# The very last store of an adaLN block, from one DMA queue to two

## Chip, core and metric

The kernel runs on one core of one Trainium2 chip (trn2). The metric is the device time of one execution in microseconds (us). Three runs of the kernel before took 598.09, 598.38 and 598.5 us; the median is 598.38 us.

## What is computed

The reference is a block with adaptive layer norm, in float32. The input x has 2 x 2048 tokens of 512 features, and each of the two sequences has one condition vector t.

```python
emb = jnp.dot(silu(t), ada_w) + ada_b
shift_msa, scale_msa, gate_msa, shift_mlp, scale_mlp, gate_mlp = jnp.split(emb, 6, axis=-1)
norm = _ln(x) * (1.0 + scale_msa[:, None]) + shift_msa[:, None]
h = gelu(jnp.dot(norm, ssm_w1) + ssm_b1, approximate=False)       # 512 -> 512
x = x + gate_msa[:, None] * (jnp.dot(h, ssm_w2) + ssm_b2)         # 512 -> 512
norm2 = _ln(x) * (1.0 + scale_mlp[:, None]) + shift_mlp[:, None]
hf = gelu(jnp.dot(norm2, ff_w1) + ff_b1, approximate=True)        # 512 -> 1024
x = x + gate_mlp[:, None] * (jnp.dot(hf, ff_w2) + ff_b2)          # 1024 -> 512
return x
```

`_ln` is the layer norm without weights: subtract the mean, multiply by the reciprocal root of the variance plus 1e-6.

## The kernel before, in words

The 4096 tokens are cut into eight blocks of 512 (`NBLK`), four to a sequence. Block i lies in SBUF as `xs[i]`, 128 partitions x 4 tokens x 512 features: partition p holds four consecutive tokens, so that a store of one token place c for all partitions writes one piece of each partition's row. The output is seen in the same way through `out_blk[i]`.

The four matrix products of each block run on TensorE by schemes that need fewer multiplications than the plain one. The products that end in a residual (`residual`, named `oA` for the first and `oC` for the second) are of Strassen's kind: seven half-sized products P1 to P7, made by `group` in the order P1, P2, P6, P5, P7, P3, P4 (`ORDER`), each of 2 x `kdim` matmuls of 128 columns by 256 (`kdim` is 4 in `oC`, so 16 matmuls per product). They accumulate in PSUM, partly on top of one another, and after each product the closure `after` lets VectorE add what stands in PSUM to a quarter of `xs[i]` (line 652). A quarter is two of the four token places by one half of the features.

The whole order of work is written out by hand (`manual_schedule`): the code issues instructions for each engine in the order of the program, and small pieces of other work (`hooks`) are placed behind chosen products. Each engine works through its own list, and waits on semaphores for the others. DMAs are issued by SyncE (queue q1 in the profile) and ScalarE (queue q10). ScalarE's DMAs are the first rows of constants, one quarter of a weight, and half of the exchange of transposed blocks (line 524). All stores of the output are SyncE's.

For blocks 0 to 6 the output is stored in two halves of 512 KB by `store` (line 675). For the last block (`last=True` in `residual`) the end is cut finer. P1, P6, P7 and P4 are taken apart by j (`parted`): the matmuls of j = 0 go to one PSUM tile and those of j = 1 to another, and `after` runs for each, with `js` the slice of one token place. Behind P7 the token places 2 and 3 of the upper half of the features are final and are stored one after the other, behind P3 the first two token places are stored by `store`, and behind P4 the token places 2 and 3 of the lower half of the features. That gives four stores of 128 KB from line 656 (128 partitions x 1 KB each), the last of which follows the last matmul and the last addition of the kernel. At the very end, the closing instructions of the program (line 1154) let SyncE wait for every DMA and bring all engines together.

Of the kernel before, what the change touches and what calls it, by code (L numbers as in the profile page):

```python
# [140 lines left out]
def kernel(  # L141
# [16 lines left out]
    nc = tc.nc  # L158
    P = 128
# [24 lines left out]
    out_blk = out.flatten_outer_dims().rearrange("(i p c) d -> i p c d", p=P, c=C)  # L184
# [230 lines left out]
    def group(name, kdim, lhs, rhs, after, hooks, parted=(), order=ORDER):  # L415

        ps = {}
        for p in order:  # L420
            b = BANK[p]
            fresh = b not in ps
            apart = p in parted
            if fresh:
                ps[b] = [
                    ps_g.tile([P, 2, HT], F32, tag=b, name=f"p{b}_{name}_{n}") for n in range(1 + apart)
                ]
            for j in range(2):
                for k in range(kdim):
                    nc.tensor.matmul(  # L430
                        ps[b][j * apart][:, j, :],
                        lhs(p, j, k),
                        rhs(p, j, k),
                        start=(fresh and j * (not apart) == 0 and k == 0),
                        stop=(p in ("P2", "P3", "P4") and k == kdim - 1),
                        skip_group_check=True,
                    )
                if apart:
                    after(p, {b: ps[b][j]}, slice(j, j + 1))
            if not apart:  # L440
                after(p, {b: ps[b][0]}, slice(0, 2))
            for op in hooks.get(p, ()):
                op()
# [194 lines left out]
    def residual(name, i, hops, wops, kdim, hooks, last=False, order=ORDER):  # L638

        xt = xs[i]  # L640
        F = D // 2
        q = {
            "11": xt[:, 0:2, :F],
            "12": xt[:, 0:2, F:],
            "21": xt[:, 2:4, :F],
            "22": xt[:, 2:4, F:],
        }
        dest = {"P1": "11", "P2": "11", "P6": "12", "P5": "22", "P7": "22", "P3": "12", "P4": "21"}

        def after(p, ps, js):  # L650
            d = q[dest[p]][:, js]
            nc.vector.tensor_tensor(d, ps[BANK[p]][:, js], d, ALU.add)  # L652
            if last and p in ("P7", "P4"):
                s = slice(2 + js.start, 2 + js.stop)
                f = slice(F, D) if p == "P7" else slice(0, F)
                nc.sync.dma_start(out=out_blk[i][:, s, f], in_=xt[:, s, f])

        parted = ("P1", "P6", "P7", "P4") if last else ()
        group(name, kdim, hops, lambda p, j, k: wops[p][:, k, :], after, hooks, parted, order)
# [499 lines left out]
```

## Time and profile before

| what | value |
|---|---|
| median of three runs | 598.38 us |
| the profiled execution's own time | 598.25 us |
| its span, first to last instruction | 596.2 us |
| TensorE busy (PE) | 589.3 us, 99% |
| VectorE, GpSimd, ScalarE busy | 373.0, 396.0, 219.8 us |
| granted TensorE clock | 1.0 |
| DMA queues q1 (SyncE) and q10 (ScalarE) | 45.11 MB and 4.22 MB |
| stores of 128 KB at line 656 | 4, each 332 to 333 ns to issue |
| ScalarE's last activation | starts 569.37 us, 0.91 us |

All times of the trace are microseconds from the start of the span. The span and the execution's own time differ by what lies around the instructions. A line of the timeline gives the start, the duration, the engine and line, the operation with the tiles it writes and reads, and in square brackets how long the engine had been idle and what ended that. Lines with "x2" merge two instructions, from the start of the first to the end of the last. SPq and ACTq are the instruction streams of SyncE and ScalarE; a DMA issue there is only the issue, and the bytes move later, on 16 DMA engines.

### The profile page before, as it was taken

The page shows a single profiled execution, that of the slowest core. Times are in us where ns is not written, and L with a number is a line of the kernel's source. Part 1 is how long each engine was busy: PE and PEld are TensorE (multiplying, and loading weights), DVE is VectorE, ACT ScalarE, POOL GpSimd, SP SyncE. Part 2 cuts the span into 40 slices and gives each one's busy share as a digit, 9 for nine tenths or more (in the row PEclk, how much of TensorE's full clock was granted, in tenths as well). Part 3 has the DMA queues.
Part 4 walks back from the last instruction along what each step waited for, and adds up shares of the span by engine and source line. Part 5 has one row for each costly group of instructions (what it writes and reads, how often), then busy time and mean ns, then how long its engine had stood idle before and what let it go on. Part 6 is the DMA issues. An engine that isn't in the chain of part 4 may idle for free.

```text
span 596.2 us, 8228 instructions
## 1 busy us (share of the span) xinstructions
PE 589.3 (99%) x2847; PEld 509.6 (85%) x2847; DVE 373.0 (63%) x638; ACT 219.8 (37%) x365; POOL 396.0 (66%) x465
## 2 busy tenths in 40 slices
PE   7999999999999999999999999999999999999997
PEld 4788888888888888888888888888888888888886
DVE  4978988897564475555754458653665246468642
ACT  3234437305432364133721356232553234212420
POOL 2878489999753994649968499966974695440200
PEclk9999999999999999999999999999999999999999
DMA  8990323200224004340042601321020300022001
GB/s 322 409 364 11 80 72 87 91 36 35 72 70 140 3 1 139 110 139 2 18 141 67 215 3 44 98 72 70 1 69 3 111 32 1 1 63 80 1 0 71
DMA packets 23481, 49.86 MB, mean 84 GB/s; under 512 B 4450, under 2 KB 5006, under 8 KB 22544
## 3 DMA queue, kind: packets, MB, share of 16 engines
q1 hardware_dynamic: 20400, 45.11, 22.5%
q10 hardware_dynamic: 3040, 4.22, 2.8%
q8 instruction: 23, 0.38, 0.3%
q14 instruction: 18, 0.15, 0.1%
HBM read 26.25 MB, written 8.39 MB: 58 GB/s over the span
## 4 chain that ended last, share of the span: by engine, by line
PE 97%; DMA 2%; DVE 1%; SPq 0%; issue 0%
PE py_oC L430 19%; PE px_hC L751 10%; PE py_oA L430 9%; PE pv_oC L430 9%; PE py_hA L430 9%; PE py_hC L751 8%; PE pv_hC L751 8%; PE pv_oA L430 5%; PE px_oC L430 5%; PE pv_hA L430 4%; PE py_hC L430 2%; PE px_oA L430 2%; PE px_hA L430 2%; DMA ada<-in_L_cond_ada_w_dram 2%; PE pv_hC L430 1%; PE pt L533 1%
## 5 line engine op out<-in xcount | busy, mean ns | idle before, releaser
L664 POOL TENSOR_TENSOR x<-x,gb 128x512 f32<-128x512 f32 x64 | 79.4, 1273 | 6.1 <-DVE gb L671 2.3
L547 ACT ACTIVATE nT<-nT,mod,mod 128x512 f32<-128x512 f32 x54 | 39.6, 802 | 105.3 <-DMA nT<-blocks 99.1
L473 POOL TENSOR_SCALAR ve<-mv 128x4 f32<-128x4 f32 x16 | 3.7, 230 | 91.3 <-DVE mv L465 85.2
L504 ACT ACTIVATE nT<-x,nmr,rstd 128x512 f32<-128x512 f32 x56 | 42.4, 803 | 51.6 <-POOL nmr L491 35.8
L430 PE MATMUL py_oC<-fw,hClo 128*128 128x256 f32 x256 | 57.9, 379 | 0.0
L430 PEld LDWEIGHTS py_oC<-fw,hClo 128*128 128x128 f32 x256 | 48.6, 190 | 6.6
L652 DVE TENSOR_TENSOR x<-py_oC,x 128x512 f32<-128x512 f32 (+1 forms) x36 | 22.6, 629 | 42.4 <-PE py_oC L430 42.4
L350 POOL TENSOR_TENSOR hSC<-hClo,hChi 128x512 f32<-128x512 f32 (+1 forms) x17 | 20.1, 1188 | 39.9 <-ACT hChi L746 29.2
L464 DVE BATCH_NORM_STATS2 st<-x 128x6 f32<-128x512 f32 x64 | 43.4, 678 | 5.0 <-DMA x<-in_x_dram 4.8
L751 PE MATMUL py_hC<-forms,fw 128*128 128x256 f32 x168 | 40.8, 379 | 0.0
L768 DVE TENSOR_TENSOR hClo<-hClo,py_hC 128x512 f32<-128x512 f32 x42 | 28.4, 680 | 16.9 <-ACT hClo L765 10.4
L515 DVE STREAM_TRANSPOSE blocks<-nT 128x512 f32<-128x512 f32 x56 | 37.8, 694 | 1.3 <-ACT nT L504 0.9
L689 POOL TENSOR_TENSOR forms<-forms 128x256 f32<-128x256 f32 x48 | 35.6, 741 | 2.8
L751 PEld LDWEIGHTS py_hC<-forms,fw 128*128 128x128 f32 x168 | 31.8, 190 | 4.4
L768 DVE TENSOR_TENSOR hChi<-hChi,pv_hC 128x512 f32<-128x512 f32 x35 | 23.3, 683 | 17.1 <-PE pv_hC L751 17.1
L652 DVE TENSOR_TENSOR x<-py_oA,x 128x512 f32<-128x512 f32 x32 | 22.0, 688 | 18.9 <-PE py_oA L430 18.3
L430 PE MATMUL py_hA<-nT,w 128*128 128x256 f32 x128 | 30.4, 380 | 0.0
L746 ACT ACTIVATE hClo<-hClo,colsT 128x256 f32<-128x256 f32 x56 | 25.4, 500 | 10.8 <-DVE hClo L768 10.7
L430 PE MATMUL py_oC<-fw_s,hSC 128*128 128x256 f32 x128 | 28.9, 379 | 0.0
L430 PE MATMUL pv_oC<-fw,hSC 128*128 128x256 f32 x128 | 28.9, 379 | 0.0
L430 PE MATMUL pv_oC<-fw_s,hSC 128*128 128x256 f32 x128 | 28.9, 379 | 0.0
L430 PE MATMUL py_oC<-fw_s,hChi 128*128 128x256 f32 x128 | 28.9, 379 | 0.0
(217 smaller groups left out, 1424.9 us busy)
## 6 DMA issues: line engine op xcount, KB each, us to landing
nT<-blocks SPq DMA_DIRECT2D x168, 64.0 KB, 2.0
out_dram<-x SPq DMA_DIRECT2D x15, 512.0 KB, 2.6
x<-in_x_dram SPq DMA_DIRECT2D x7, 1024.0 KB
ada<-in_L_cond_ada_w_dram SPq DMA_DIRECT2D x6, 1024.0 KB, 15.8
fw<-in_L_cond_ff_w_dram SPq DMA_DIRECT2D x3, 2048.0 KB
nT<-blocks ACTq DMA_DIRECT2D x56, 64.0 KB, 2.0
w<-in_L_cond_ssm_w_dram SPq DMA_DIRECT2D x3, 1024.0 KB, 9.5
x<-in_x_dram SPq DMA_DIRECT2D x2, 512.0 KB, 4.0
```

What stands on the lines that cost most here:

```text
L350: eng.tensor_tensor(out[:, r], a[:, r], b[:, r], f)
L430: nc.tensor.matmul(ps[b][j * apart][:, j, :], lhs(p, j, k), rhs(p, j, k), start=(fresh and j * (not apart) == 0 and k == 0), stop=(p in (" ...
L464: nc.vector.bn_stats(st, xs[self.i][:, c, :])
L504: nc.scalar.activation(t, x_c, AF.Identity, bias=self.nmr[:, c : c + 1], scale=self.rstd[:, c : c + 1])
L515: nc.vector.transpose(self.bl[:, :, :, c, :].rearrange("p m k q -> p k m q"), self.nT[:, c, :].rearrange("p (k m q) -> p k m q", k=KD, m=C),)
L547: nc.scalar.activation(dst, src, AF.Identity, bias=shift, scale=scale)
L652: nc.vector.tensor_tensor(d, ps[BANK[p]][:, js], d, ALU.add)
L664: lambda c=c: nc.gpsimd.tensor_tensor(xs[i][:, c, :], xs[i][:, c, :], gb, ALU.add)
L689: eng.tensor_tensor(reg[d], reg[a], reg[b], ALU.add if f == "+" else ALU.subtract)
L746: nc.scalar.activation(h, h, AF.Gelu_apprx_tanh, bias=fb1T[:, m : m + 1])
L751: nc.tensor.matmul(ps[b][:, j, :], fa[ra][:, j * P : (j + 1) * P], fb[rb].rearrange("p a (c q) -> p c a q", q=Q), start=(fresh and j == 0) ...
L768: nc.vector.tensor_tensor(dest(d), dest(d), ps[b], op)
```

## The change

The store behind P7 and the first of the two behind P4 stay as they are. The second one behind P4 (`js.start` is 1: the last store of all) becomes two stores of 64 partitions x 1 KB: partitions 0 to 63 issued by SyncE, partitions 64 to 127 issued by ScalarE. Both wait for the same addition of VectorE. No other instruction is added, removed or moved; all later lines of the code are numbered 5 higher (656 becomes 661, 675 becomes 680, 1154 becomes 1159).

```diff
             if last and p in ("P7", "P4"):
                 s = slice(2 + js.start, 2 + js.stop)
                 f = slice(F, D) if p == "P7" else slice(0, F)
-                nc.sync.dma_start(out=out_blk[i][:, s, f], in_=xt[:, s, f])
+
+                queues = (nc.sync, nc.scalar) if p == "P4" and js.start else (nc.sync,)
+                n = P // len(queues)
+                for e, eng in enumerate(queues):
+                    r = slice(e * n, (e + 1) * n)
+                    eng.dma_start(out=out_blk[i][r, s, f], in_=xt[r, s, f])
```

## The prediction

> **What bounds the kernel now.** I read the page first: the busy row of TensorE, and the chain that ended last.
>
> ```profile
> span 596.2 us, 8228 instructions
> PE 589.3 (99%) x2847; PEld 509.6 (85%) x2847; DVE 373.0 (63%) x638; ACT 219.8 (37%) x365; POOL 396.0 (66%) x465
> ...
> PE 97%; DMA 2%; DVE 1%; SPq 0%; issue 0%
> ```
>
> TensorE is busy for 99% of the span and 97% of the chain is matmul. The change touches none of that: it rewrites one DMA behind the last matmul. So only the tail can move, and I read the end of the timeline next (start, duration, engine, line).
>
> ```profile
> 589.16 3.62 PE L430 MATMUL py_oC<-fw_s,hChi 128*128 128x256 f32 x16
> ...
> 591.54 2.06 SPq L656 DMA_DIRECT2D out_dram<-x  x2
> 592.82 0.42 DVE L652 TENSOR_TENSOR x<-py_oC,x 128x256 f32<-128x256 f32 x1 [1.30 <-PE py_oC L430]
> ```
>
> The last addition ends at 592.82 + 0.42 = 593.24. The two merged stores end at 591.54 + 2.06 = 593.60, and one issue takes 332 ns, so the last store is issued from 593.27. The tail from there is 596.23 - 593.27 = 2.96 us, 0.5% of the span. I cut it by the DMA's own rows (each line: stretch, length, busy time by engine, clock, DMA share, GB/s), and look at what SyncE waits for at the very end and where the closing instructions of the program (line 1154) stand.
>
> ```profile
> 593.27:593.60 0.33, 0.00 (x0) 0.00 (x0) 0.00 (x0) 0.00 (x0) 0.00 (x0) 1.00 0.00 0
> 593.60:594.10 0.50, 0.00 (x0) 0.00 (x0) 0.00 (x0) 0.00 (x0) 0.00 (x0) 1.00 0.00 0
> 594.10:594.55 0.45, 0.00 (x0) 0.00 (x0) 0.00 (x0) 0.00 (x0) 0.00 (x0) 1.00 0.83 291
> 594.55:595.15 0.60, 0.00 (x0) 0.00 (x0) 0.00 (x0) 0.00 (x0) 0.00 (x0) 1.00 0.00 0
> 595.15:596.23 1.08, 0.00 (x0) 0.00 (x0) 0.00 (x0) 0.00 (x0) 0.00 (x0) 1.00 0.00 0
> ```
>
> ```profile
> SPq L1154 <- DMA out_dram<-x: 1.5, 1, 1.5
> ```
>
> ```profile
> L1154 SPq EVENT_SEMAPHORE  x7: 17/28/28, 595.2 to 596.2; - x7
> L1154 POOLq EVENT_SEMAPHORE  x4: 17/17/17, 595.6 to 596.1; - x4
> ```
>
> So the tail is: 0.33 issue, 0.50 until the first byte moves, 0.45 in which 128 KB move, 0.60 until SyncE is told, 1.08 of closing waits and the barrier of all engines. Only 0.45 us of it depends on bytes. A perfect halving of that would be worth 0.22 us, or 0.04% of the time.
>
> **The change part by part.** Before the tail nothing moves: on TensorE, VectorE and GpSimd the order of instructions is the same but for line numbers, SyncE has the same stores up to the last, and ScalarE has two instructions more, at its end.
>
> *SyncE's half.* One store of 128 partitions becomes one of 64, waiting on the same addition. Taken at the same 0.33 issue and 0.50 start-up: on SyncE the 512 KB store at 590.08 and the 128 KB stores have the same issue time (332 ns), so bytes do not set it. Whether fewer partitions shorten it no row shows for a store; the nearest, a 32-partition copy quoted below, has a longer issue (about 0.5 us) and moves its first byte 1.17 us after it begins, not earlier. So I take nothing saved. The other end: if the 0.50 halved with the partitions, 0.25 us saved. The form differs, so that end stays in the range.
>
> *ScalarE's half.* ScalarE ends its last activation at 569.37 + 0.91 = 570.28 and is then idle, so its wait for the addition holds up nothing but its own closing branch, drain and barrier signal, for which GpSimd collects from 595.6 on. ScalarE's issue would end by about 594.2 even at the longest of the rows below (0.86 us), so 1.4 us cover it; without that cover each us would be a us of time. Its wait is a semaphore instruction of its own followed by the DMA, as in SyncE's store of the addition at 585.91, which ends at 586.33 and whose store issues at 584.67 + 2.06 - 0.33 = 586.40: 0.07 after the addition, against 0.03 for the last store. So ScalarE issues 0.04 later, about 593.31.
>
> *The two together.* The trace has a place where SyncE and ScalarE issue in the same moment: the exchange of the transposed blocks, 64 KB each. First the timeline, then the DMA queues of the two next stretches, 532.12 to 532.44 and 532.44 to 532.76.
>
> ```profile
> 530.95 1.15 SPq L524 DMA_DIRECT2D nT<-blocks  x2
> 530.96 1.42 ACTq L524 DMA_DIRECT2D nT<-blocks  x2
> ```
>
> ```profile
> q1 hardware_dynamic: 34, 0.06, 76.6%
> ```
>
> ```profile
> q10 hardware_dynamic: 33, 0.06, 84.9%
> q1 hardware_dynamic: 14, 0.00, 5.4%
> ```
>
> From 530.9 to 532.12 no packet moves. Then q1 (SyncE's) moves its 64 KB in 0.32 us, and ScalarE's q10 moves none until 532.44. Issued 0.01 later, it starts 0.32 later. The pair at 179.16 and 179.17 shows the same: q1 from 180.33, q10 from 180.65. ScalarE's second issue is stretched too: the two SyncE issues take 512 and 583 ns, the two of ScalarE 523 and 864.
>
> Here the Trainium skill speaks against the change. Its page "DMA: Bandwidth & Descriptors", section "Rules for kernel authors", says not to bother with two transfers to disjoint partition halves, since both use the same 16 engines and their packets only interleave. By that rule the sum is 128 KB over the same engines: the same 0.45 us, and a difference of 0 to +0.04 us from ScalarE's later issue. The row says a little worse: no interleaving, one behind the other. If the 0.32 us is a delay in starting the second transfer, ScalarE's half starts at 594.10 + 0.32 = 594.42 and takes half of 0.45, so it ends at 594.64, which is 0.09 us behind the 594.55 of before. If the 0.32 us is only the time that the first one's bytes took, the wait scales with SyncE's half (0.22) and the end stays at 594.55. The rows don't separate these. I take +0.09, because the row is this very pair of queues, and the stretched second issue speaks for a shared step ahead of the bytes. The bounds: -0.25 (start-up scales with partitions), and 0.09 + (0.864 - 0.523) = +0.43 if ScalarE's half also meets the stretched issue.
>
> *The closing waits.* SyncE's list of waits has the same length; it waits first on the semaphore that ScalarE's half now counts, then on its own. The 1.08 us follow whichever lands last, so I cost this at nothing. It is a plain addition to the path: nothing covers a later landing.
>
> **Sum.** The profiled execution took 598.25 us, its span 596.23, with 2.02 us around it. 598.25 + 0.09 = 598.34. It lies 0.13 below the median of 598.38, so on that scale the forecast is 598.47, rounded to 598.5.
>
> **The rivals.** *It does nothing* (the halves interleave, as the rule has it): 598.38 to 598.42. For it: bytes and engines are the same. Against it: the 0.32 us of the row.
>
> *It helps*: with 64 partitions per queue the 0.50 us ahead of the first byte shortens, down to 598.38 - 0.25 = 598.13. For it: this stretch is dead time in which two queues might work at once. Against it: the 32-partition copy starts no sooner. To win over 0.2% (1.2 us) it would have to remove more than a third of a tail of which the closing 1.08 and the landing's 0.60 are not touched; hardly possible.
>
> *ScalarE's half meets the stretched issue*: 598.38 + 0.43 = 598.81. For it: the 864 ns. Against it: that was a second issue, and here there is one per queue.
>
> *Slower by over 0.2%: ScalarE's new instructions are not at hand when the addition ends.* The page's instruction queue, q8, has 23 packets that take 0.3% of 16 engines' span: 0.003 x 16 x 596.2 / 23 = 1.24 us each. A fetch is itself a transfer; with the 0.60 us that a store needs to be told, I estimate 1.24 + 0.60 = 1.84 us. If it fell between ScalarE's wait and its issue, the issue would come at 593.31 + 1.84 = 595.15, the first byte 0.83 later at 595.98, the last at 596.20: 1.65 us behind 594.55, or 600.0 us. It decides from the point where ScalarE issues later than 594.42 - 0.83 = 593.59; from there each us counts in full. Against it: ScalarE has 23 us of idle time before, and VectorE's closing drain is listed at the same 592.8 as its last addition, so it passed from the one to the other without a fetch.
>
> **How the numbers follow.** Second half delayed by a start-up, +0.09: 0.50. Nothing, 0 to +0.04: 0.27. A gain of up to 0.25: 0.13. Stretched issue, up to +0.43: 0.05. A fetch or another late arrival of ScalarE, about +1.65: 0.05. The runs of before spread over 598.09 to 598.5, about 0.2 either way. The range reaches from 598.13 less this spread, about 598.0, to 598.81 plus it, 599.0. A measurement of this kernel can tell about 0.2% (1.2 us) from no change; all but the last case lie within that. Slower by more: 0.05. Faster by more: 0.01, taken from the gain case for what I overlook. Within: 0.94.
>
> **What would show it.** In the profile after: TensorE's last matmul and VectorE's last addition at the same times as before within the spread (else something moved that I say does not). Two issues of line 661, on SPq at about 593.27 and on ACTq at about 593.31, with some 0.33 us each. No byte before 594.10; q1 with 64 KB first, q10 with 64 KB from 594.42 if the start-up is shared, both from about 594.10 if they interleave; the last byte near 594.6. SyncE's closing wait ends near 595.2 and the closing instructions take 1.08 as before. The prediction is wrong if the first byte comes clearly sooner than 0.83 after the issue, if ScalarE issues later than 593.59, or if the closing part grows, for instance through ScalarE arriving at the barrier after 595.6.

## The result and the profile after

The changed kernel takes 599.1 us in the median of 22 runs (598.67 to 601.39), the kernel before 598.49 us in 22 runs beside it: 0.61 us more. The ratio is 1.0016 with a 95% interval of 1.001 to 1.0022. That is slower, by less than the 0.2% that I had set as the bound of a change, and 0.1 us above the upper end of my range. A repeat on another occasion (e12 below) gave 1.0011, 1.0002 to 1.0019. The ratio of 1.0016 is more than 0.61 us would make (1.0010), since 7 of these 22 runs were a microsecond or more longer, at a granted clock of 0.997, as by their times were 2 of the 22 of before; in the repeat 1 run of 14 showed that clock.

The two profiled executions took 599.0 us (span 596.90) and 598.25 us (span 596.23). The page after says as before that TensorE is the chain.

```profile
span 596.9 us, 8230 instructions
...
PE 97%; DMA 2%; DVE 1%; SPq 0%; issue 0%
```

The end of the timeline after:

```profile
592.88 0.42 DVE L652 TENSOR_TENSOR x<-py_oC,x 128x256 f32<-128x256 f32 x1 [1.30 <-PE py_oC L430]
593.39 0.55 ACTq L661 DMA_DIRECT2D out_dram<-x  x1
```

The last addition ends at 593.30, 0.06 later than before, within the spread of runs. From there to the end of the span before took 596.23 - 593.24 = 2.99 us, and after it takes 596.90 - 593.30 = 3.60. The difference of 0.61 us is the whole loss, and it lies behind the last addition. This stretch, from the end of the last addition to the end of the span, is what I call the tail below. The issues of the stores after, from the view of the tensor `out_dram` (minimum, median and maximum in ns):

```profile
L661 SPq DMA_DIRECT2D out_dram<-x x4: 332/332/538, 584.7 to 593.3; - x4
...
L661 ACTq DMA_DIRECT2D out_dram<-x x1: 552/552/552, 593.4 to 593.4; - x1
```

Three of SyncE's four still take 332 ns; the one of 64 partitions takes 538, and ScalarE's 552. The tail cut as before (stretch, length, then busy times, clock, DMA share and GB/s):

```profile
593.33:593.87 0.54, 0.00 (x0) 0.00 (x0) 0.00 (x0) 0.00 (x0) 0.00 (x0) 1.00 0.00 0
593.87:594.52 0.65, 0.00 (x0) 0.00 (x0) 0.00 (x0) 0.00 (x0) 0.00 (x0) 1.00 0.00 0
594.52:595.25 0.73, 0.00 (x0) 0.00 (x0) 0.00 (x0) 0.00 (x0) 0.00 (x0) 0.91 0.70 180
595.25:595.82 0.57, 0.00 (x0) 0.00 (x0) 0.00 (x0) 0.00 (x0) 0.00 (x0) 0.50 0.00 0
595.82:596.90 1.08, 0.00 (x0) 0.00 (x0) 0.00 (x0) 0.00 (x0) 0.00 (x0) 0.50 0.00 0
```

To compare the third stretch, the prediction's division of the tail has to be set right: it ended the moving of the bytes at 594.55, but the last packets of the kernel before end just short of 594.60. In this line of before the share of the DMA engines is still 0.03, and nothing follows it.

```profile
594.55:594.60 0.05, 0.00 (x0) 0.00 (x0) 0.00 (x0) 0.00 (x0) 0.00 (x0) 1.00 0.03 0
```

Measured to the end of the last packet in both, the issue went from 0.33 to 0.54, the wait for the first byte from 0.50 to 0.65, the moving of the bytes from 0.50 to 0.73, the time until SyncE is told from 0.55 to 0.57, and the closing part stayed at 1.08. By queue, first 594.51 to 594.79, then 594.79 to 595.25:

```profile
q1 hardware_dynamic: 52, 0.05, 73.3%
```

```profile
q10 hardware_dynamic: 80, 0.07, 54.6%
q1 hardware_dynamic: 28, 0.01, 11.4%
```

SyncE's queue begins alone, and ScalarE's first byte comes 0.28 us after it, while SyncE's bytes still move. So two things lie open: why SyncE's half moves its first byte 0.36 us later after its issue began than the whole store did (1.19 against 0.83), and what the second queue adds.

### The profile page after: what moved, and what is told of

It is laid out like the page before. It is cut to its first block, busy times and chain, and to the rows that moved or that the text cites. A ratio compares the mean times of both kernels' runs of the same rounds, so it can differ in the third digit from the quotient of the medians.

```text
span 596.9 us, 8230 instructions
## 1 busy us (share of the span) xinstructions
PE 588.7 (99%) x2847; PEld 509.3 (85%) x2847; DVE 373.3 (63%) x638; ACT 219.8 (37%) x365; POOL 396.5 (66%) x465
## 4 chain that ended last, share of the span: by engine, by line
PE 97%; DMA 2%; DVE 1%; SPq 0%; issue 0%
PE py_oC L430 19%; PE px_hC L756 10%; PE py_oA L430 9%; PE pv_oC L430 9%; PE py_hA L430 9%; PE py_hC L756 8%; PE pv_hC L756 8%; PE pv_oA L430 5%; PE px_oC L430 5%; PE pv_hA L430 4%; PE py_hC L430 2%; PE px_hA L430 2%; PE px_oA L430 2%; DMA ada<-in_L_cond_ada_w_dram 2%; PE pv_hC L430 1%; PE pt L533 1%
## 5 line engine op out<-in xcount | busy, mean ns | idle before, releaser
L430 PE MATMUL px_oC<-fw,hChi 128*128 128x256 f32 x128 | 28.9, 379 | 0.0
```

Of the source, the lines that this page charges most:

```text
L430: nc.tensor.matmul(ps[b][j * apart][:, j, :], lhs(p, j, k), rhs(p, j, k), start=(fresh and j * (not apart) == 0 and k == 0), stop=(p in (" ...
```

## The experiments

All times in the text are medians in us; the time of before is that of the same series. Tails are from the profile of each kernel.

**e1, e2, e3, e4: the second queue or the half store?** My first theory was that a store of 64 partitions is slow by itself, the rival that two queues which issue in the same moment slow each other. e1 leaves both halves to SyncE:

```diff
-                nc.sync.dma_start(out=out_blk[i][:, s, f], in_=xt[:, s, f])
+                very_last = p == "P4" and js.start
+                for r in (slice(0, 64), slice(64, P)) if very_last else (slice(0, P),):
+                    nc.sync.dma_start(out=out_blk[i][r, s, f], in_=xt[r, s, f])
```

> The two halves by partitions stay, but SyncE issues both, one behind the other; ScalarE has no part in it. Theory 1 (a 64-partition store is slow by itself: 0.54 us to issue and 1.20 us to the first byte, where the 128-partition store has 0.33 and 0.83): the first half issues in 0.54 and moves its first byte 1.20 after its issue begins; the second issues some 0.6 later and lands about 2.0 after that, so the end comes about 0.6 to 0.8 us later than before. Theory 2 (two queues that issue in the same moment slow each other): with one queue both halves issue in 0.33 and the first byte comes at 0.83; the second half lands some 0.2 us later than before.

Measured: 599.37 against 598.5, ratio 1.0017 (1.001 to 1.0023), tail 3.89. The issues take 536 and 588 ns and the first byte comes 1.19 after the first of them began. SyncE is told of the second half 0.97 us later behind the addition than of the whole store before. The first theory holds, though its cost was put too low (0.6 to 0.8).

e2 keeps the two queues and cuts by features:

```diff
-                nc.sync.dma_start(out=out_blk[i][:, s, f], in_=xt[:, s, f])
+                very_last = p == "P4" and js.start
+                parts = ((nc.sync, slice(0, 128)), (nc.scalar, slice(128, F))) if very_last else ((nc.sync, f),)
+                for eng, c in parts:
+                    eng.dma_start(out=out_blk[i][:, s, c], in_=xt[:, s, c])
```

> Both queues issue in the same moment as in the changed kernel, but the store is cut by features and not by partitions: 128 partitions x 512 bytes each. Theory 1 (partition count): both issues take 0.33 us, the first byte comes 0.83 after, ScalarE's bytes about 0.3 behind SyncE's, so the end is 0.1 to 0.3 us later than before. Theory 2 (two queues in the same moment): issues of about 0.54 us and first bytes at 1.2 and 1.4 as in the changed kernel, the end about 0.6 us later than before.

Measured: 598.52 against 598.5, ratio 0.9998 (0.9989 to 1.0008), tail 3.07, 0.08 more than before. The end of its timeline:

```profile
593.02 0.42 DVE L652 TENSOR_TENSOR x<-py_oC,x 128x256 f32<-128x256 f32 x1 [1.30 <-PE py_oC L430]
593.47 0.33 SPq L659 DMA_DIRECT2D out_dram<-x  x1
593.53 0.39 ACTq L659 DMA_DIRECT2D out_dram<-x  x1
```

Two queues in the same moment, and the issues take 0.33 and 0.39, the first byte comes 0.83 after SyncE's issue began and ScalarE's 0.19 later. The rival falls: the slow issue does not come from the second queue.

e3 gives the whole store to ScalarE:

```diff
-                nc.sync.dma_start(out=out_blk[i][:, s, f], in_=xt[:, s, f])
+                very_last = p == "P4" and js.start
+                eng = nc.scalar if very_last else nc.sync
+                eng.dma_start(out=out_blk[i][:, s, f], in_=xt[:, s, f])
```

> The last store stays whole, 128 partitions, but ScalarE issues it instead of SyncE. By theories 1 and 2 alike its issue takes 0.33 us, it begins 0.03 to 0.07 later than SyncE's did, and the first byte comes 0.83 after it: the end 0.04 us later than before, no measurable difference. If ScalarE's queue is slow by itself (theory 3), its issue takes about 0.55 and the first byte 1.2 to 1.4: the end 0.4 to 0.6 us later.

Measured: 598.31 against 598.5, ratio 0.9995 (0.9987 to 1.0004), tail 3.11. Its issue takes 392 ns and the first byte comes 0.90 after: ScalarE's queue is 0.06 us slower than SyncE's, not 0.2 or more, and that is not seen in the time.

e4 makes only SyncE's half and leaves the other 64 partitions of that store out:

```diff
-                nc.sync.dma_start(out=out_blk[i][:, s, f], in_=xt[:, s, f])
+                very_last = p == "P4" and js.start
+                r = slice(0, 64) if very_last else slice(0, P)
+                nc.sync.dma_start(out=out_blk[i][r, s, f], in_=xt[r, s, f])
```

> Leaves out part of the output: only SyncE's half of the last store is made (partitions 0 to 63), the rows of partitions 64 to 127 of that store are never written. Theory 1 (partition count): issue 0.54, first byte at 1.20, so with half the bytes the landing still comes about 0.15 us later than the whole store's before. Theory 2 (two queues): alone on its queue the half issues in 0.33, its first byte comes at 0.83 and it lands about 0.2 us earlier than the whole store did.

Measured: 598.92 against 598.5, ratio 1.0009 (1.0003 to 1.0016), tail 3.30. The stretches of issue, start-up and bytes in its tail:

```profile
593.44:593.97 0.53, 0.00 (x0) 0.00 (x0) 0.00 (x0) 0.00 (x0) 0.00 (x0) 1.00 0.00 0
593.97:594.63 0.66, 0.00 (x0) 0.00 (x0) 0.00 (x0) 0.00 (x0) 0.00 (x0) 1.00 0.00 0
594.63:595.09 0.46, 0.00 (x0) 0.00 (x0) 0.00 (x0) 0.00 (x0) 0.00 (x0) 1.00 0.56 143
```

Half of the bytes alone are slower than all of them in one store: the start costs 0.36 us more, and the moving takes 0.45 us for 64 KB (from the first packet to the last; the stretch shown is 0.01 wider) where 128 KB took 0.50. So of the 0.61 us, SyncE's half alone brings 0.31 (tail 3.30 against 2.99), and ScalarE's half the other 0.30 (3.60).

**e5, e6, e7, e9, e10, e14, e15, e16: which stores are slow?** These are probes. The last store stays whole, and the stores behind P7 (and in two of them the one behind P3), which land before the last store is issued, are given other shapes. Each ran once, for its profile. The edit is of this form, here e5:

```diff
-                nc.sync.dma_start(out=out_blk[i][:, s, f], in_=xt[:, s, f])
+                parts = (slice(0, P),)
+                if p == "P7":
+                    parts = (slice(64, P), slice(0, 64)) if js.start else (slice(0, 96), slice(96, P))
+                for r in parts:
+                    nc.sync.dma_start(out=out_blk[i][r, s, f], in_=xt[r, s, f])
```

> A probe off the path: the last store is whole again, and the two 128 KB stores behind P7, whose bytes have moved long before the end, are cut by partitions on SyncE's queue: the first into 96 and 32, the second into partitions 64 to 127 and then 0 to 63. Theory 1a (every store of fewer than 128 partitions takes the slow way): the 96-partition store and the 64-partition store that starts at partition 64 both take 0.53 to 0.55 us to issue, as partitions 0 to 63 did, and 1.19 to the first byte. Theory 1b (the cost rises as the count falls): 96 lies between 0.33 and 0.54, 32 above it. The time as before within 0.2 us by both.

> A probe off the path: the last store is whole; the two stores behind P7 become two stores of 64 partitions x 2 token places x 1 KB, issued one after the other behind the second addition, so that each has 128 pieces, as many as the fast store of 128 partitions x 1 KB. Theory 1a (128 partitions are what counts): issue 0.5 us or more, first byte at about 1.2. Theory 1c (128 pieces are what counts): issue 0.33, first byte at 0.83. The time as before within 0.2 us by both.

> A probe off the path: the last store is whole; the two stores behind P7 are cut by partitions on SyncE's queue, the first into 112 and 16, the second into 120 and 8. Theory 1a (any count but 128 takes the slow way): issues of 0.53 us or more for 112 and 120. Theory 1b (cost rises as the count falls): 112 and 120 lie near 0.33 to 0.36. The time as before within 0.2 us by both, unless a store of 120 partitions is so slow that it delays the queue.

> A probe off the path: the last store is whole; the two stores behind P7 are cut by partitions on SyncE's queue, the first into 80 and 48, the second into 72 and 56. So far 96, 112, 120 and 128 partitions issued in 0.33 to 0.35 us, 64 in 0.53. If the slow way begins right at 64, both 80 and 72 take 0.33 to 0.35; if the cost climbs between 96 and 64, 80 takes about 0.43 and 72 about 0.48. The time as before within 0.3 us.

> The same probe with 65 and 63 partitions for the first store behind P7 and 48 and 80 for the second. If the slow way begins right at 64, 65 partitions issue in 0.33 to 0.35 us and 48 in 0.53 or more; if the cost climbs as the count falls, 65 lies at 0.53 and 48 above it, at 0.6. The time as before within 0.3 us.

> A probe off the path: the last store is whole; the two stores behind P7 are cut by partitions on SyncE's queue, the first into 32 and 96, the second into 16 and 112. If only counts that are a power of two below 128 are slow, 32 and 16 partitions both take 0.5 us or more to issue and 1.15 to 1.2 to the first byte, as 64 did; if 64 is slow alone, they take 0.3 and 0.8 as 48 did.

> A probe off the path that leaves out part of the output: the last store is whole, but of the stores behind P7 the first writes only 64 partitions x 512 bytes and the second only 56 partitions x 1 KB, and the store behind P3 only 32 partitions x 2 KB; the rest of these three is never written. If 64 partitions are slow whatever the length of the rows, the first takes 0.53 us to issue and 1.19 to the first byte; if 64 KB in all is what counts (64 x 1 KB and the exchange's 32 x 2 KB were slow), the first is fast and the third is slow. 56 is expected fast (0.33 and 0.82).

> A probe off the path that leaves out part of the output: the last store is whole, but of the stores behind P7 the first writes only partitions 32 to 95 and the second only partitions 0 to 59, and the store behind P3 only 64 partitions x 4 KB; the rest of these three is never written. If 64 partitions are slow wherever they lie and whatever the length of the rows, the first and the third take 0.53 us to issue and 1.19 to the first byte; if it is 64 KB in all, the third is fast. 60 is expected fast.

Read were the issue and the first byte of the first store behind each addition; a second one right behind another waits for it and says nothing (32 partitions took 636 ns to issue behind the 96 of e5, and 345 by themselves in e14). Where the pair before had bytes still moving when the issue began (120, 72, 48 and 16 partitions, and the 64 from partition 64), these had ended before the first byte. Two lines of e5, the 96-partition store and the 64-partition store that begins at partition 64:

```profile
L660 SPq DMA_DIRECT2D out_dram<-x x1: 347/347/347, 584.6 to 584.6; - x1
```

```profile
L660 SPq DMA_DIRECT2D out_dram<-x x1: 532/532/532, 586.3 to 586.3; - x1
```

All of them together, in ns (the first byte counted from the begin of the issue):

| partitions x row | kernel | issue | first byte |
|---|---|---|---|
| 128 x 1 KB | before | 332 | 833 |
| 120 x 1 KB | e7 | 339 | 811 |
| 112 x 1 KB | e7 | 347 | 846 |
| 96 x 1 KB | e5 | 347 | 845 |
| 80 x 1 KB | e9 | 347 | 852 |
| 72 x 1 KB | e9 | 313 | 785 |
| 65 x 1 KB | e10 | 353 | 824 |
| **64 x 1 KB**, from 64 / from 32 | e5 / e16 | 532 / 551 | 1193 / 1212 |
| **64 x 512 B** | e15 | 532 | 1191 |
| **64 x 4 KB** | e16 | 520 | 1179 |
| **64 x 2 rows of 1 KB** | e6 | 718 | 1377 |
| 60 x 1 KB | e16 | 367 | 838 |
| 56 x 1 KB | e15 | 359 | 832 |
| 48 x 1 KB | e10 | 323 | 812 |
| 32 x 1 KB / 32 x 2 KB | e14 / e15 | 345 / 334 | 845 / 833 |
| 16 x 1 KB | e14 | 314 | 817 |

All three of my rules fell in turn: that every count below 128 is slow (96 is fast), that it begins at 64 and goes on below (48 is fast), that powers of two are slow (32 and 16 are fast). The total of 64 KB is not it either (32 x 2 KB is fast, 64 x 512 B slow), nor the number of pieces (64 x 2 rows has 128 and is slow), nor the place of the partitions. Of the counts read, only 64 is slow, in every form. The eight runs took 597.98 to 598.71, within 0.4 of before.

The probes also tell something of the bytes. Here are two stores of 64 partitions x 1 KB, both slow to start, with no other bytes moving beside theirs: first the one from partition 64 in e5, then the one from partition 32 in e16.

```profile
587.50:587.95 0.45, 0.45 (x4) 0.40 (x3) 0.00 (x0) 0.00 (x0) 0.00 (x0) 1.00 0.57 146
```

```profile
586.19:586.52 0.33, 0.33 (x3) 0.28 (x3) 0.30 (x1) 0.00 (x0) 0.00 (x0) 1.00 0.58 199
```

The same 64 KB take 0.45 us from partitions 64 to 127, as in e4 from 0 to 63, and 0.33 from 32 to 95 in the one run that has this store. So the slow moving of the halves goes with which partitions are taken and not with their number alone; why, no run shows.

**e13: the change with another cut.** Partition 80 in place of 64, all else as in the change:

```diff
-                nc.sync.dma_start(out=out_blk[i][:, s, f], in_=xt[:, s, f])
+                very_last = p == "P4" and js.start
+                parts = ((nc.sync, slice(0, 80)), (nc.scalar, slice(80, P))) if very_last else ((nc.sync, slice(0, P)),)
+                for eng, r in parts:
+                    eng.dma_start(out=out_blk[i][r, s, f], in_=xt[r, s, f])
```

> The change as it is, two queues and a cut by partitions in the same moment, but at partition 80 instead of 64: SyncE stores partitions 0 to 79, ScalarE 80 to 127. Alone on the queue, stores of 48 and of 80 partitions issued in 0.32 and 0.35 us and moved their first byte 0.81 and 0.85 after. If the loss comes from the count of 64, both issues take 0.32 to 0.4 here, the first byte comes 0.85 after SyncE's issue and ScalarE's some 0.1 to 0.2 behind, and the end is 0 to 0.1 us later than before: 598.4 to 598.5. If it comes from a cut by partitions over two queues, the end is 0.6 us later as in the changed kernel: 599.1.

Measured: 598.49 against 598.56, ratio 1.0002 (0.9994 to 1.001), tail 3.19.

```profile
593.12 0.35 SPq L659 DMA_DIRECT2D out_dram<-x  x1
593.18 0.37 ACTq L659 DMA_DIRECT2D out_dram<-x  x1
```

Two queues, a cut by partitions, and the loss is gone from the median. In the trace 0.20 us of it stay: ScalarE's first byte comes 0.27 after SyncE's and its bytes take 0.4. The time does not resolve that.

**e17: the mark.** I then compared the instructions as built, and found that each DMA carries a field, `ant_dge_precooked`. It is set on every store of the kernel before and on all stores of the table but those of 64 partitions. It is missing there, on four very small copies, and on the 224 copies of the transposed blocks (168 of SyncE and 56 of ScalarE, whose part is a quarter and not the half named above), whose issue is slow too (507 ns at the least). What sets it I did not find out. The language lets one keep a DMA from being marked, so the mark can be taken off the fast store:

```diff
+                nc.dge_precook = not (p == "P4" and js.start)
                 nc.sync.dma_start(out=out_blk[i][:, s, f], in_=xt[:, s, f])
+                nc.dge_precook = True
```

> The kernel before with one thing altered: the last store, whole, 128 partitions, on SyncE's queue, is built without the mark (ant_dge_precooked) that the built program puts on every store of the kernel before, and on the stores of 8, 16, 32, 48, 56, 60, 63, 65, 72, 80, 96, 112 and 120 partitions of the probes, but on none of 64 partitions and none of the exchange's copies. If the missing mark is the cause, the whole store takes 0.53 us to issue and 1.19 to the first byte, and its landing comes about 0.36 us later: 598.8 to 598.9 against 598.5. If it is the count of 64 itself and the mark only goes along with it, the store issues in 0.33 and the time is as before.

Measured: 598.88 against 598.6, ratio 1.0009 (0.9997 to 1.002), tail 3.37. The time alone would not decide it; the profile does:

```profile
594.24:594.79 0.55, 0.00 (x0) 0.00 (x0) 0.00 (x0) 0.00 (x0) 0.00 (x0) 1.00 0.00 0
594.79:595.45 0.66, 0.00 (x0) 0.00 (x0) 0.00 (x0) 0.00 (x0) 0.00 (x0) 1.00 0.00 0
595.45:595.96 0.51, 0.00 (x0) 0.00 (x0) 0.00 (x0) 0.00 (x0) 0.00 (x0) 1.00 0.74 257
```

A whole store of 128 partitions, with nothing changed but the mark, has the slow issue of 0.55 and the first byte at 1.21, and its tail is 0.38 longer than that of before. Its bytes take 0.49 from the first packet to the last, against 0.50, so the mark does not bear on them. Taking the mark off makes the start slow, and each 64-partition store of these kernels lacks it: that is the cause of the slow start. The other direction, a store of 64 partitions with the mark, was not tried.

**e8, e11: the closing list.** SyncE's closing instructions read the completion semaphores of the DMAs, in an order that was the same in every kernel. In the kernel before, the last store's was in the first of five, so the other four followed its landing, about 62 ns apart. In e8 four half stores of earlier blocks are cut in two, so that the last store counts on the semaphore read last; in e11 four stores are merged away to the same end.

```diff
+        if i in (1, 2, 3):
+            if not half:
+                return
+            s = slice(0, C)
         nc.sync.dma_start(out=out_blk[i][:, s, :], in_=xs[i][:, s, :])
```

(e11, in `store`; its two stores behind P7 are one as well.)

> The whole last store of before, but the four half stores of blocks 1 and 2 are each cut into two stores of one token place (128 partitions x 2 KB), so that four more completion semaphores of the ring of eight are used up and the last store counts on the one that SyncE's closing list reads last. Before, the last store's semaphore was read first, and four more semaphore instructions of 62 ns each followed its landing. If these are what the closing part is made of, they now pass while the last store is under way: 4 x 0.062 = 0.25 us less, 598.25 against 598.5. Rival: the closing part is set by the barrier of the engines or by the drains, and nothing is saved: 598.5.

> The late semaphore a second time, by four stores fewer instead of four more: blocks 1, 2 and 3 are stored whole (1 MB) instead of in halves, and the two stores behind P7 become one of 256 KB; the last store stays whole and alone and counts on the semaphore that is read last. The run with four stores more reached the first barrier 0.25 us sooner and lost 0.16 of it to SyncE's second drain, which came late. If that lateness came with the four instructions more, the full 0.25 is saved here: 598.1 to 598.25 against 598.4. If it belongs to the late semaphore itself, 0.1 is saved.

Measured: e8 598.1 against 598.37, ratio 0.9997 (0.9989 to 1.0006), tail 2.91; e11 597.97 against 598.5, ratio 0.9993 (0.9983 to 1.0002), tail 2.74. The closing instructions of SyncE in e8 and in e11, to be held against the 595.2 to 596.2 of before:

```profile
L1158 SPq EVENT_SEMAPHORE  x7: 17/28/28, 593.5 to 596.0; - x7
L1158 SPq DRAIN  x3: 7/7/130, 595.1 to 595.7; - x3
```

```profile
L1161 SPq EVENT_SEMAPHORE  x7: 17/28/28, 595.2 to 597.4; - x7
L1161 SPq DRAIN  x3: 7/7/7, 596.7 to 597.0; - x3
```

Four of the five now pass while the store is on its way. e8 gives 0.16 of the 0.25 back to a late second drain (130 ns, and late to begin); in e11 all drains take 7 ns and the tail is 0.25 shorter than before. Five of the probes bear the order out: with two stores more (e5, e7, e9, e10, e14) the last store counts on the semaphore that the third instruction reads, and their tails are all 2.91, against 2.99 to 3.02 in e6, e15 and e16. So the tail can be cut by 0.25 us, in the trace; both intervals hold 1, so that e11 beats the kernel before is not shown by the times. Its median fell by 0.53, more than its tail; the rest is not explained, and neither is why e8's drain was late.

**e12: the change once more.**

> The changed kernel once more, on the same chip as the others of this call. If the whole loss is the 0.62 us by which its store lands later, its median is 0.6 above that of before, ratio 1.0010, and runs with a mean clock of 0.997 are no more frequent than in the other kernels (16 of 103 so far in the other kernels and before). If the change also made those runs more frequent (7 of 22 in its first measurement), a third of its runs shows that clock again and the ratio is about 1.0016.

Measured: 599.21 against 598.5, ratio 1.0011 (1.0002 to 1.0019), tail 3.59. The loss repeats, 0.71 us in the median and 0.60 in the tail, the excess in the first ratio does not. (The 16 of 103 in that expectation should read 20 of 158.)

## Why the prediction was wrong

Right were: TensorE and all up to the last addition unmoved; ScalarE free, its issue 0.06 after SyncE's (I had 0.04), its arrival at the barrier covered; SyncE first and ScalarE behind it; the time until SyncE is told (0.57 against 0.55) and the closing 1.08 hardly changed; slower and within 0.2%.

Wrong was the first step of the change part by part, *SyncE's half*, "taken at the same 0.33 issue and 0.50 start-up". It took 0.54 and 0.65: 0.36 us more. The row that told this was before me: the exchange's copy, with "a longer issue (about 0.5 us)" and its first byte 1.17 after. I set it aside because its form differs, and gave the other end of this term only a gain. That the 512 KB and the 128 KB stores issue alike did show that bytes do not set the issue, but both have 128 partitions and both carry the mark, so it said nothing of the new form. By that row the term should have run from -0.25 to 1.17 - 0.83 = +0.34; with the stretched issue on top the range would have reached 598.38 + 0.43 + 0.34, about 599.2. That the missing mark was the reason could not be read from any row.

The other term, *the two together*, was right in taking a delay of ScalarE's start and not a wait for the end of SyncE's bytes (it began 0.28 behind, SyncE's bytes took 0.45), and mis-sized in one part. I put ScalarE's start 0.32 behind SyncE's; it was 0.28. I put the moving of half the bytes at half of 0.45; in the change each half takes 0.45, and so it does alone in e4. So in place of 0.32 + 0.22 - 0.45 = +0.09 stands, with the whole store's bytes at 0.50, 0.28 + 0.45 - 0.50 = +0.23. With the 0.36 of the start and 0.02 until SyncE is told, that is the 0.61 of the tail. That 598.5 missed by only 0.6 is owed to the small tail, in which no term is large, and not to these two.

On the rule of the Trainium skill against two halves by partitions ("DMA: Bandwidth & Descriptors", "Rules for kernel authors"): its advice holds here. The sum of 0 to +0.04 that I drew from it is near the +0.08 measured where both parts have the fast start (e2, cut by features), less so the +0.20 of the cut at partition 80 (e13). The shared engines that it gives as the reason are not the main cause of the loss here: 0.36 of the 0.61 us lie ahead of the first byte.

The rivals that end later did not come: no fetch of instructions on ScalarE, which began its issue at 593.39, and no stretched issue, since ScalarE's took 552 ns against the 538 of SyncE's, and SyncE's alone in e4 took 0.53.

Not settled: why 64 partitions go unmarked, why 64 KB take 0.45 us from some partitions and 0.33 from others, and what share of the 0.28 between the queues is a shared step. The delay is there with fast starts as well (0.19 in e2, 0.27 in e13). As an estimate, 0.06 of it is ScalarE's later issue and 0.07 its slower start when it is alone (0.90 against 0.83, e3), which leaves 0.15 for the change, 0.06 in e2 and 0.14 in e13.

## What to carry to other kernels

A store at the very end is nearly all fixed cost: here 0.50 of 2.99 us were bytes, so cutting it can win little, and each new form of the DMA must first be held against the old one's issue time. A DMA whose issue takes 0.5 us where its like takes 0.33 is worth a look at how it was built: stores of 64 partitions were slow where those of 48, 80 and 128 were not. And when a row near to the case is slower than the value one takes, its number is the bound, whatever speaks for the difference.

## What the runs showed of the hardware that was not expected

- A store of 64 partitions x 1 KB moves its first byte 0.36 us later than one of 128 (1.19 against 0.83), and with rows of 512 bytes and 4 KB it is the same, while all other counts that were read, from 16 to 128, issue in 0.31 to 0.37. Taking the mark off a 128-partition store gives it the same slow start (1.21).
- 64 KB from partitions 0 to 63 (e4) or 64 to 127 (e5) took 0.45 us to move, from 32 to 95 (e16) 0.33, and 128 KB from all 128 took 0.50.
- The order in which the closing list reads the semaphores is worth up to 0.25 us at the end of a kernel (tail 2.74 in e11 against 2.99).
